# Extra TensorE products ahead of the gathered sums of a four-layer vision block

## The chip, the cores and the metric

The kernel is one program on one core of a Trainium2 chip. The metric is the device time of that core in microseconds (us), as the median of several runs. TensorE is called PE here, VectorE DVE, ScalarE ACT, GpSimd POOL and SyncE SP, as in the profile.

## The reference

Four images of 256 channels by 64x64 pixels, all in float32, go through four residual layers; ahead of each layer the image is normalised in groups of 8 channels (`_gn`).

```python
x = x + L0(_gn(x))   # 1x1 convolution, deformable 3x3 sampling (4 groups, 9 points), SE gate, MLP
x = x + L1(_gn(x))   # qkv, a 5x5 depthwise branch, linear attention, projection
x = x + L2(_gn(x))   # 3x3 convolution with binarised weights
x = x + L3(_gn(x))   # non-local attention over a 2x2 max-pooled image
```

The part that matters here is the sampling of layer 0. For each pixel, group and point the reference reads four neighbouring pixels at a computed place, weighs them bilinearly, multiplies by a softmax mask and adds the nine points:

```python
samp = _grid_sample(img, sg)                       # 4 corners x bilinear weights
dout = (samp * mask).sum(-1)                       # over the 9 points
dout = einsum('nhwc,oc->nhwo', dout, outproj_w)    # 1x1 projection, then a batch norm
```

## The kernel before

**Stages.** `run` (L1218) first convolves image 0, then runs four samplings, one an image, one after the other. Beside each sampling other work is laid in: beside the first (image 0) the convolutions and the sampling offsets of images 1 to 3 (`convolve`, `offsets`); beside the second the binarised weights, then `feedforward` and `layer1` of image 0; beside the third and the fourth `feedforward` and `layer1` of the image before, and `layer2` and `layer3` of the image two before. After the samplings comes what is left of the last images.

**A sampling** (`sample`, L558) goes in 16 blocks of 18 rounds, 288 rounds in all. In a round, `gathered` (L592) issues four indirect DMAs on POOL (one a group, L596, each with 128 rows of 256 floats into a tile `g`, of which there are seven), and 8 matmuls on PE (L603) that multiply the gathered rows with a sparse weight tile `wm` into `acc`. These 8 matmuls are "the sums". The profile has each float32 matmul twice, so a round's sums are 16 records there. `acc` is one PSUM bank: two halves of 256 columns, used in turn by pairs of rounds; an even round writes the first 128 columns of its half, the odd round the other 128.

After an odd round, ACT copies its half out (`moved`, L608, into `at`) in the next round; PE transposes it (`turned`, L613, into `dp`) in the round after that; ACT spreads it into `dT` (`spread`, L623). After a block, `project` (L636) makes 8 matmuls, two groups of 4, six to eight rounds later. ACT also makes the weight tiles `wm` (L588) for the rounds to come.

**The order** on PE, DVE, ACT and POOL is the order in which the program emits (`manual_schedule`). A helper, `beside` (L1234), takes one round of the sampling and then as much of the other work as is due, so a round's place on PE is: what is due of `turned` and `project`, the sums, then the other work that falls into this round. The first matmul of an even round's sums waits for ACT's copy of the pair before, since both are in the same PSUM bank.

```python
for i in range(NBLK * BR):
    b, r = divmod(i, BR)
    for f in later.pop(i, ()):
        f()
    if r % UR == 0:                       # UR = 2: a pair of rounds
        acc = next(accs)
    gathered(blocks[b], weights[0][0], acc, r)
```

Of the kernel before, what the change touches and what calls it, by code (L numbers as in the profile page):

```python
# [17 lines left out]
P = 128  # L18
# [24 lines left out]
STEPS = 900  # L43
CONV, SECOND = NB * 22.5 + 11, 568
# [27 lines left out]
class Net:  # L72
    def __init__(self, ctx, tc, a, out):
# [5 lines left out]
        self.banks, self.alone, self.spare = cycle(["mm"]), False, False  # L79
        self.dp = e(tc.tile_pool(name="scratch", bufs=1, space=DRAM))  # L80


# [29 lines left out]
    def groupnorm(self, pool, st, name):  # L112
# [7 lines left out]
        nc.tensor.matmul(pg[:, 0:KT], self.bd8, mv[:, :, 0], start=True, stop=True)  # L120
# [8 lines left out]
        nc.tensor.matmul(pv[:, 0:KT], self.bd8, d, start=True, stop=True)  # L129
# [6 lines left out]
    def folded(self, pool, out, w, sc, bi, name):  # L136
# [5 lines left out]
        for m in range(n):  # L142
            for k in range(KT):
                nc.tensor.matmul(ps[:, m:m + 1], w[:, k, m * P:(m + 1) * P], bi[:, k:k + 1], start=k == 0, stop=k == KT - 1)
# [109 lines left out]
    def binarise(self):  # L254
# [4 lines left out]
        with self.tc.tile_pool(name="bin", bufs=1, side="left") as sp, \  # L259
# [17 lines left out]
            for i in range(6):  # L277
                nc.tensor.matmul(ps[:, 0:C], self.ones, sums[:, i], start=i == 0, stop=i == 5)
# [27 lines left out]
    def weights(self, pool):  # L306
# [7 lines left out]
        for m in range(KT):  # L314
            dg = pool.tile([P, P], F32, name=f"dg{m}")
            nc.vector.tensor_scalar(dg, self.ident, self.inv[:, m:m + 1], None, ALU.mult)
            nc.tensor.matmul(ps[:, m * P:(m + 1) * P], self.ones, dg, start=True, stop=True)
# [4 lines left out]
    def convolve(self, n, w, sp, bp, pads, used):  # L322
# [47 lines left out]
        def convolved(b, x, yb, m):  # L370
            ps = self.ps1.tile([P, 512], F32, name="cv", tag="vk")
            for k in range(KT):
                nc.tensor.matmul(ps, cw[:, k, m * P:(m + 1) * P], x[:, k], start=k == 0, stop=k == KT - 1)
# [13 lines left out]
        def projected(b, x, yb, xo, j2):  # L387

            ps = self.ps().rearrange("p (r o) -> p r o", o=C)
            for r in range(2):  # L390
                for h in range(2):
                    at = (4 * h + 2 * j2 + r) * W
                    for k in range(KT):
                        nc.tensor.matmul(ps[64 * h:64 * h + 64, r], yb[:, k, at:at + W], w["iw"][:, k], start=k == 0, stop=k == KT - 1)
# [81 lines left out]
    def offsets(self, n, c, y, mw, bp, used):  # L476
# [14 lines left out]
        for h in range(2):  # L491
            ps = self.ps().rearrange("p (j o) -> p j o", o=P)
            for j in range(4):
                at = (4 * h + j) * P
                for k in range(KT):
                    nc.tensor.matmul(ps[:, j, 0:3 * Q], t[:, k, at:at + P], mw[:, k], start=k == 0, stop=k == KT - 1)
# [61 lines left out]
    def sample(self, n, ssum):  # L558
# [33 lines left out]
        def gathered(sl, wm, acc, r):  # L592
# [8 lines left out]
            for x in range(2):  # L601
                for i in range(G):
                    nc.tensor.matmul(acc[32 * i:32 * i + 32, :], wm[:, r4, 4 * i + 2 * x:4 * i + 2 * x + 2, :],  # L603
# [29 lines left out]
        def project(b, m):  # L633
            po[m] = self.ps("po")
            for k in range(G):
                nc.tensor.matmul(po[m][:, 0:BR * OB], self.ow[:, k, m * P:(m + 1) * P], dT[b][:, k].rearrange("p r o -> p (r o)"), start=k == 0, stop=k == G - 1)  # L636
# [19 lines left out]
        for i in range(NBLK * BR):  # L656
# [3 lines left out]
            if r % UR == 0:  # L660
                acc = next(accs)
            gathered(blocks[b], weights[0][0], acc, r)
            if r == 0 and b + 1 < NBLK:
# [22 lines left out]
    def feedforward(self, n, ssum, st):  # L686
        nc, tc, a = self.nc, self.tc, self.a
        with tc.tile_pool(name=f"fa{n}", bufs=1, side="right") as sp, \
# [13 lines left out]
            for k in range(KT):  # L702
                nc.tensor.matmul(ps[0:64, 0:1], sd[:, k], mean[:, k:k + 1], start=k == 0, stop=k == KT - 1)
# [4 lines left out]
            for m in range(KT):  # L708
                ps = self.ps()
                nc.tensor.matmul(ps[:, 0:1], su[:, m * P:(m + 1) * P], dn, start=True, stop=True)  # L710
# [673 lines left out]
```

## Time and profile before

| | |
|---|---|
| median of 3 runs | 8691.39 us (8685.18 to 8699.55) |
| profiled execution, its own time | 8695.07 us |
| span of its profile | 8693.3 us |
| granted TensorE clock, mean over the span | 0.803 |
| sums of sampling 1 / 2 / 3 / 4 on PE | from about 140 / 1934 / 3659 / 5449 us, the last to 7210 us |
| busy in the span | PE 5880.0, DVE 4817.7, ACT 3541.0, POOL 4934.7 us |

The span is the time from the first to the last instruction of the profiled execution; the 1.8 us around it belong to that execution's own time. "PEclk" is the share of the full TensorE clock that was granted. A group's row has the busy time, the mean duration in ns, and the idle time of its engine just before it with what ended it. "remote" (in the chain: "another core or an unknown queue") is a wait whose releasing event has no instruction beside it in the records; as there is one core, it is no other core here. Samplings are counted from 1 in the text; in the code they are `n` = 0 to 3.

### The profile page before, as it was taken

The page shows a single profiled execution, that of the slowest core. Times are in us where ns is not written, and L with a number is a line of the kernel's source. Part 1 is how long each engine was busy: PE and PEld are TensorE (multiplying, and loading weights), DVE is VectorE, ACT ScalarE, POOL GpSimd, SP SyncE. Part 2 cuts the span into 40 slices and gives each one's busy share as a digit, 9 for nine tenths or more (in the row PEclk, how much of TensorE's full clock was granted, in tenths as well). Part 3 has the DMA queues.
Part 4 walks back from the last instruction along what each step waited for, and adds up shares of the span by engine and source line. Part 5 has one row for each costly group of instructions (what it writes and reads, how often), then busy time and mean ns, then how long its engine had stood idle before and what let it go on. Part 6 is the DMA issues. An engine that isn't in the chain of part 4 may idle for free.

```text
span 8693.3 us, 99761 instructions
## 1 busy us (share of the span) xinstructions
PE 5880.0 (68%) x35776; PEld 3498.6 (40%) x35776; DVE 4817.7 (55%) x6045; ACT 3541.0 (41%) x10767; POOL 4934.7 (57%) x4870
## 2 busy tenths in 40 slices
PE   4454554448744446688876676888766778986899
PEld 2232222224323222234644443345544333664476
DVE  5344442443366667324776675228766762699833
ACT  2333333234444433334445443444454442456414
POOL 2666666466666666666666556666655560476410
PEclk7676766669866667799988887999878879998899
DMA  6454554444533334444543344445433342220131
GB/s 172 129 160 123 145 149 118 114 143 148 158 107 106 110 109 126 137 127 138 142 133 111 111 116 138 146 135 142 141 105 111 112 118 96 74 72 29 44 97 54
DMA packets 744383, 1031.75 MB, mean 119 GB/s; under 512 B 354128, under 2 KB 459984, under 8 KB 742352
## 3 DMA queue, kind: packets, MB, share of 16 engines
q0 software_dynamic: 221184, 604.27, 24.4%
q1 hardware_dynamic: 522704, 421.10, 16.4%
q8 instruction: 283, 4.64, 0.2%
q14 instruction: 212, 1.74, 0.1%
HBM read 856.39 MB, written 168.61 MB: 118 GB/s over the span
## 4 chain that ended last, share of the span: by engine, by line
PE 43%; another core or an unknown queue 17%; DVE 17%; ACT 13%; issue 8%; DMA 1%; POOL 0%; SPq 0%; ACTq 0%; DVEq 0%; POOLq 0%
DVE agg L178 10%; PE acc L603 6%; PE ps L739 5%; PE ps L749 5%; ACT wm L588 5%; PE ps L1085 4%; PE ps L821 3%; PE ps L943 2%; PE ps L1203 2%; PE s L1185 2%; PE po L636 2%; ACT dT L623 2%; ACT at L608 1%; PE rden L934 1%
## 5 line engine op out<-in xcount | busy, mean ns | idle before, releaser
L596 POOL DMA_INDIRECT g<-tab,sl x4608 | 4399.0, 955 | 2790.8 <-issue 1179.7
L178 DVE SCALAR_TENSOR_TENSOR agg<-pad,vec,agg 128x1024 f32<-128x1024 f32 x2280 | 2934.5, 1287 | 63.9
L603 PE MATMUL acc<-g,wm 128*32 128x128 f32 x18432 | 1012.4, 336 | 2022.6 <-ACT at L608 1471.8
L603 PEld LDWEIGHTS acc<-g,wm 128*32 128x32 f32 x18432 | 557.7, 129 | 2524.7 <-ACT at L608 1683.4
L588 ACT ACTIVATE wm<-sl,con 128x48 f32<-128x48 f32 x6144 | 1490.1, 366 | 26.0 <-remote 12.6
L1085 PE MATMUL ps<-xd,w 128*128 128x256 f32 x3072 | 741.0, 392 | 37.6 <-issue 30.1
L623 ACT COPY dT<-dp 64x128 f32<-64x128 f32 x1152 | 297.2, 258 | 985.8 <-remote 524.3
L1085 PEld LDWEIGHTS ps<-xd,w 128*128 128x128 f32 x3072 | 587.3, 196 | 159.0 <-issue 79.0
L739 PE MATMUL ps<-x2f,f 128*128 128x512 f32 x1024 | 502.3, 639 | 10.2 <-issue 5.1
L608 ACT COPY at<-acc 128x256 f32<-128x256 f32 x576 | 214.5, 372 | 712.8 <-remote 607.4
L821 PE MATMUL ps<-xr,qw 128*128 128x512 f32 x768 | 463.5, 733 | 21.8 <-issue 8.5
L724 DVE SCALAR_TENSOR_TENSOR hm<-ps,vec,lk 128x512 f32<-128x512 f32 x256 | 190.6, 750 | 502.4 <-ACT lk L741 375.2
L749 PE MATMUL ps<-hm,f 128*128 128x512 f32 x1024 | 463.6, 601 | 0.0
L741 ACT ACTIVATE lk<-ps,low 128x512 f32<-128x512 f32 x256 | 174.0, 687 | 514.7 <-PE ps L739 413.2
L636 PE MATMUL po<-dT,ow 128*128 128x288 f32 x1024 | 336.7, 477 | 56.5 <-issue 13.8
L875 ACT COPY kt<-pt 128x512 f32<-128x512 f32 x256 | 149.5, 585 | 544.8 <-remote 246.8
L1036 POOL TENSOR_TENSOR xd<-xp 128x640 f32<-128x640 f32 x64 | 79.8, 1275 | 497.3 <-DMA xq<-x 280.3
L1203 PE MATMUL ps<-gt,pT 128*128 128x129 f32 x2048 | 316.5, 315 | 47.1 <-ACT pT L1199 32.9
L613 PE MATMUL dp<-ident,at 128*128 128x128 f32 x1152 | 285.5, 336 | 77.1 <-ACT dT L623 53.4
L1203 PEld LDWEIGHTS ps<-gt,pT 128*128 128x128 f32 x2048 | 297.2, 226 | 98.8 <-ACT pT L1199 45.0
L1185 PE MATMUL s<-ph,th 128*128 128x512 f32 x512 | 289.2, 677 | 42.9 <-DVE ot L938 9.2
L739 PEld LDWEIGHTS ps<-x2f,f 128*128 128x128 f32 x1024 | 199.2, 203 | 253.3 <-issue 238.5
(243 smaller groups left out, 7710.6 us busy)
## 6 DMA issues: line engine op xcount, KB each, us to landing
g<-tab,sl POOLq DMA_INDIRECT x4608
x<-x SPq DMA_DIRECT2D x128, 512.0 KB
xr<-x SPq DMA_DIRECT2D x96, 512.0 KB
tab<-xo SPq DMA_DIRECT2D x192, 128.0 KB
x<-in_x SPq DMA_DIRECT2D x32, 512.0 KB
y<-yc SPq DMA_DIRECT2D x32, 512.0 KB
yb<-y SPq DMA_DIRECT2D x64, 256.0 KB
x<-yb SPq DMA_DIRECT2D x64, 256.0 KB
```

The source lines that it names most:

```text
L178: nc.vector.scalar_tensor_tensor(to, s, wt, acc, ALU.mult, ALU.add)
L588: nc.scalar.activation(wm[:, :, :, o], blocks[b][:, r:r + WR, G:], AF.Copy, scale=self.con("own")[:, o:o + 1])
L596: nc.gpsimd.indirect_dma_start(out=g[:, i, :], out_offset=None, in_=table, in_offset=bass.IndirectOffsetOnAxis(ap=sl.bitcast(I32)[:, r, i: ...
L603: nc.tensor.matmul(acc[32 * i:32 * i + 32, :], wm[:, r4, 4 * i + 2 * x:4 * i + 2 * x + 2, :], g[:, i, x * P:(x + 1) * P], start=x == 0, st ...
L623: nc.scalar.copy(dT[b][hs, :, r:r + UR], dp[u][hs, :, :, s, :].rearrange("p v g o -> p g v o"))
L636: nc.tensor.matmul(po[m][:, 0:BR * OB], self.ow[:, k, m * P:(m + 1) * P], dT[b][:, k].rearrange("p r o -> p (r o)"), start=k == 0, stop=k ...
L739: nc.tensor.matmul(ps, f1[:, k, m * P:(m + 1) * P], x2[:, k], start=k == 0, stop=k == KT - 1)
L749: nc.tensor.matmul(ps, f2[:, k, m * P:(m + 1) * P], hm[:, k], start=k == 0, stop=k == 4 * KT - 1)
L821: nc.tensor.matmul(ps, qw[:, k, m * P:(m + 1) * P], x[:, k], start=k == 0, stop=k == KT - 1)
L1085: nc.tensor.matmul(ps[:, e], w[:, k, t, 2 * half + e, m * P:(m + 1) * P], v[:, 2 * half + e, k, t:t + 8], start=i % 6 == 0, stop=i % 6 == 5)
L1185: nc.tensor.matmul(s[i], tv[:, 4 * b + j], ph[:, i * 512:(i + 1) * 512], start=True, stop=True)
L1203: nc.tensor.matmul(ps[:, 0:P + 1], pT[:, m], gt[:, m], start=m == 0, stop=m == 7)
```

## The change

A counter `self.work` adds up the PE work that is emitted: a helper `of` wraps the output of every `matmul` call (not of the transposes) and adds twice its columns, scaled by the share of the 128 partitions that it writes. In the first two samplings (`n < 2`), ahead of a round's sums, PE multiplies the constant identity matrix with a part of the constant weight tile `ow`, into the part of `acc` from the round's own columns to the end of its half, until the counter has reached `ALIVE = 2048`. The sums then overwrite these values. After the sums the counter is set to 0. So a round in which other work of 2048 or more was emitted since the last sums gets no extra product, and a round with none gets 2048 of it: 4 products of 256 columns in an even round (512 each), 8 of 128 columns in an odd one (256 each).

```diff
+ALIVE = 2048
...
-        self.banks, self.alone, self.spare = cycle(["mm"]), False, False
+        self.banks, self.alone, self.spare, self.work = cycle(["mm"]), False, False, 0
...
+    def of(self, out):
+
+        self.work += 2 * out.size() // P
+        return out
...
-                nc.tensor.matmul(ps, cw[:, k, m * P:(m + 1) * P], x[:, k], start=k == 0, stop=k == KT - 1)
+                nc.tensor.matmul(self.of(ps), cw[:, k, m * P:(m + 1) * P], x[:, k], start=k == 0, stop=k == KT - 1)
...
             if r % UR == 0:
                 acc = next(accs)
+            while n < 2 and self.work < ALIVE:
+                free = acc[:, r % UR * P:]
+                nc.tensor.matmul(self.of(free), self.ident, self.ow[:, 0, 0:free.shape[1]], start=True, stop=True)
             gathered(blocks[b], weights[0][0], acc, r)
+            self.work = 0
```

The third line pair stands for the same edit at every other `matmul` call of the kernel; it emits nothing of its own.

## The prediction

> **What bounds the kernel now.** I read the page first, for the clock.
>
> ```profile
> PEclk7676766669866667799988887999878879998899
> ```
>
> Each digit is one fortieth of the span (217 us). Slices 1 to 9 and 12 to 16, the first sampling and the later part of the second, have 6 or 7 tenths of the clock; from slice 19 on it is mostly 8 or 9. The table by stage says more (columns: stretch, its length, busy time of PE, weight loads, DVE, ACT and POOL with instruction counts, clock, DMA share, GB/s).
>
> ```profile
> 280.00:1900.00 1620.00, 773.00 (x6110) 437.94 (x6102) 663.87 (x936) 549.53 (x2042) 1007.48 (x1048) 0.67 0.48 135
> 2000.00:2400.00 400.00, 311.51 (x1742) 152.11 (x1741) 148.72 (x220) 172.69 (x572) 252.62 (x261) 0.89 0.49 150
> 2400.00:3600.00 1200.00, 630.66 (x4518) 341.95 (x4518) 797.84 (x757) 466.41 (x1658) 779.94 (x822) 0.68 0.40 112
> ...
> 4400.00:5300.00 900.00, 616.64 (x4205) 381.34 (x4202) 652.66 (x748) 425.26 (x1345) 536.28 (x565) 0.82 0.41 120
> ```
>
> In the first sampling (first row) PE is busy 773 of 1620 us at clock 0.67, and no other engine is full: POOL 62%, DVE 41%, ACT 34%. So it is bound by waits. The chain of waits, cut to the samplings 1, 2 and 3, says which:
>
> ```profile
> by line: another core or an unknown queue 39.9%; ACT wm L588 9.8%; issue 9.5%; DVE agg L178 7.3%; PE acc L603 4.9%; PE ps L496 3.5%; PE cv L373 2.7%; PE ps L394 2.7%; ACT dT L623 2.2%; ACT at L608 1.8%; PE po L636 1.6%; ACT t L484 1.1%; PE
> by line: another core or an unknown queue 28.5%; ACT wm L588 8.3%; PE acc L603 7.9%; issue 7.9%; PE ps L739 6.8%; PE ps L749 6.2%; PE ps L821 4.2%; PE ps L943 3.1%; ACT dT L623 2.7%; DVE agg L178 2.5%; PE po L636 2.4%; ACT at L608 2.4%; PE
> by line: DVE agg L178 11.5%; another core or an unknown queue 8.8%; PE acc L603 8.0%; issue 7.8%; PE ps L739 6.1%; PE ps L749 5.9%; PE ps L1085 5.7%; PE ps L821 5.0%; PE ps L943 3.5%; ACT wm L588 2.9%; PE s L1185 2.8%; PE ps L1203 2.8%; PE
> ```
>
> The unknown queue holds 39.9% of 1794 us = 716 us in sampling 1, 28.5% of 1725 us = 492 us in sampling 2, and only 8.8% of 1790 us = 158 us in sampling 3. What it is, the timeline shows:
>
> ```profile
> 864.87 1.08 PE L603 MATMUL acc<-g,wm 128*32 128x128 f32 x16
> ...
> 876.83 0.37 ACT L608 COPY at<-acc 128x256 f32<-128x256 f32 x1 [8.59 <-remote]
> ...
> 877.26 1.08 PE L603 MATMUL acc<-g,wm 128*32 128x128 f32 x16 [11.31 <-ACT at L608]
> ```
>
> The odd round's sums are issued from 864.87 and their records end at 865.95, yet ACT's copy of them starts at 876.83, after 8.59 us of idle ACT, and PE's next sums start behind the copy after 11.31 us. PE tells of its end some 10 us late. I read the unknown queue as such late ends of PE work; what makes them late the trace doesn't tell. POOL and the sums in samplings 1 and 2 (busy, mean ns | idle before, by releaser):
>
> ```profile
> L596 POOL DMA_INDIRECT g<-tab,sl x1168 | 1123.4, 962 | 672.2 <-issue 311.5 <-remote 211.5 <-PE acc L603 120.0
> L603 PE MATMUL acc<-g,wm 128*32 128x128 f32 x4608 | 305.7, 370 | 871.5 <-ACT at L608 569.1 <-issue 267.1 <-DMA g<-tab,sl 22.5
> L596 POOL DMA_INDIRECT g<-tab,sl x1163 | 1110.4, 955 | 611.2 <-issue 299.9 <-remote 148.3 <-PE acc L603 99.9
> L603 PE MATMUL acc<-g,wm 128*32 128x128 f32 x4608 | 258.0, 353 | 592.8 <-ACT at L608 476.6 <-issue 86.0 <-ACT lk L741 12.5
> ```
>
> POOL waits 672.2 - 311.5 = 361 us and 611.2 - 299.9 = 311 us for more than its own issue gap, mostly for PE to free a `g` tile. A round takes 1794/288 = 6.2 and 1725/288 = 6.0 us; POOL alone needs 4 x (955 + about 300 ns) = 5.0 us. So PE and ACT in their turn set the pace, and POOL follows up to seven rounds ahead.
>
> **What the skill says.** The Trainium skill, "TensorE: Matmul & The Clock Gate", section "Part 1: The HAM clock gate", says that the array runs at half clock by default, that a window of about 3.4 us with sustained activity gives the full clock, and that an idle window takes it away. The trace agrees, and is sharper. Consecutive windows of 3.41 us (second number after the length: PE busy; then the same columns as above):
>
> ```profile
> 854.07:857.49 3.42, 1.82 (x17) 1.10 (x18) 0.00 (x0) 2.22 (x9) 2.62 (x3) 0.50 0.58 174
> 857.49:860.90 3.41, 3.41 (x10) 1.22 (x12) 0.00 (x0) 0.00 (x0) 2.03 (x3) 0.50 0.36 97
> 860.90:864.31 3.41, 1.20 (x33) 0.73 (x33) 0.00 (x0) 1.57 (x7) 1.44 (x2) 1.00 0.16 44
> ...
> 901.86:905.27 3.41, 3.41 (x19) 1.65 (x20) 0.00 (x0) 3.41 (x15) 2.50 (x4) 0.50 0.26 77
> 905.27:908.69 3.42, 1.76 (x20) 0.66 (x18) 0.00 (x0) 0.82 (x4) 1.01 (x2) 1.00 0.26 77
> 908.69:912.10 3.41, 2.35 (x32) 1.60 (x32) 1.62 (x2) 3.07 (x10) 2.77 (x3) 1.00 0.27 77
> ```
>
> At 0.50 a window with 1.82 us of PE work is followed by 0.50, full ones (3.41 us) by 1.00; at 1.00 a window with 1.76 us of work keeps it, and the 1.20 us of 860.90 lose it. Half clock needs twice the time for the same work, so both say: about 1.5 us of full-clock work in 3.4 us. I go by this. The second page is "PSUM — Partial Sum Buffer", section "Terms": two engines must not be in one bank and quadrant at once. The wait shown above (sums behind the copy) is its price here: PE's sums waited 569.1 us for L608 in sampling 1. The extra products of an even round write the same bank, so they stand behind the same wait and cannot fill it.
>
> **The change, part by part.** (1) The counter emits nothing: 0 us. (2) *How many products.* I went through PE's order from sums to sums and added up 2 x columns x partitions/128 of each matmul between. Roughly checked by groups: in sampling 1 L394 (384 matmuls x 256), L373 (96 x 1024), L496 (240 x 216) and L636 (120 x 576) make 317,600, or 1,100 a round, in lumps: 152 of 288 rounds have none, 112 have 2048 or more. Sampling 1 gets products in 176 rounds: 327 of 256 columns and 658 of 128. Sampling 2: 152 rounds, 247 and 506. (3) *Price of one.* No row is the same product; the nearest by columns are these, whose busy time per record is the pace in a dense stretch near full clock:
>
> ```profile
> L1085 PE MATMUL ps<-xd,w 128*128 128x256 f32 x3072 | 741.0, 392 | 37.6 <-issue 30.1
> ...
> L1203 PE MATMUL ps<-gt,pT 128*128 128x129 f32 x2048 | 316.5, 315 | 47.1 <-ACT pT L1199 32.9
> ```
>
> 741.0/3072 = 0.241 us a record, two records: 0.48 us for 256 columns. 316.5/2048 = 0.155, so 0.31 us for 128 columns (L1203 has 129). At full clock: sampling 1, 327 x 0.48 + 658 x 0.31 = 361 us; sampling 2, 247 x 0.48 + 506 x 0.31 = 276 us. At half clock twice that: 722 and 551 us. I take a fifth of it at half clock, since a lump of products fills a window: 433 and 331 us.
>
> (4) *How much of it is on the path.* PE is idle about half the time, but the products come behind the copy and ahead of the sums; queued behind them on PE are the sums, then the laid-in matmuls and transposes, and ACT's copy, DVE, and POOL's gather seven rounds on wait for those. Of the sums' busy time the chain holds 4.9% of 1794 = 88 of 305.7 us (0.29) in sampling 1, and 7.9% of 1725 = 136 of 258.0 us (0.53) in sampling 2. The work just ahead of the sums is on the path in the same share: 433 x 0.29 + 331 x 0.53 = 126 + 175 = 301 us. Where it is hidden, PE's idle time hides it; with no cover the price is 764 us.
>
> (5) *What the clock gives back.* A round of 6 us holds 1.8 windows. At least 2048 of extra or other work (4 records of 512 columns; the chain has 16 such records of L749 in 7.06 us, so 1.8 us) plus the sums (0.65 us for 16 records at full clock in the timeline) make 2.4 us a round, or 1.4 us a window: near what the rows above need, so some windows turn and some don't. I estimate the clock to go from 0.65 to about 0.76 in sampling 1 and from 0.74 to 0.82 in sampling 2. PE work on the chain (sums, L496, L373, L394, L636: 15.4% of 1794 = 276 us; in sampling 2 sums, L739, L749, L821, L943, L636: 30.6% of 1725 = 528 us) shrinks by about 14% and 10%: 39 + 53 = 92 us.
>
> (6) No DMA is added, and SP and POOL get no instruction; the gathers keep their order on POOL. Samplings 3 and 4 and the rest are as before: 0 us. The late ends (716 + 492 us) I leave as they are, because the trace has them inside full-clock windows too. Their bounds are the first and third rivals.
>
> Sum: 8695 + 301 - 92 = 8904 us against the profiled execution's own time; that is 4 us above the median, so 8900 us.
>
> **Rivals.**
> *Late ends go away (faster).* By stage they are rare where PE is dense: 158 us of the chain in sampling 3, whose row 4400 to 5300 has clock 0.82. If the products bring the first two samplings there, up to 716 + 492 - 2 x 158 = 892 us leave the chain, but POOL cannot gain more than the 361 + 311 = 672 us that it waits. A quarter to a half of that gives 8691 - 168 = 8520 to 8691 - 336 = 8355 us; I take 8480. For it: density and late ends go together from stage to stage. Against: the late end shown follows a PE that had worked, and within sampling 1 I find no fewer behind busier stretches.
> *All hidden.* The products fall into PE's idle half and the clock pays for the rest: 8691 us. Against: even rounds have them behind the copy.
> *The clock stays low (the change doesn't do what it says).* The products stand in one lump, windows between lumps are empty; half clock all through: 722 x 0.29 + 551 x 0.53 = 501, so 9190 us. The same comes out if PE's slow stretches stay: at 919 to 926 us its timeline has single L496 matmuls 0.7 to 1.4 us apart with no wait; 16 records at 0.7 us are 11 us a round, and 45 such rounds of 328 add 500 us. It decides from some 20 such rounds on.
>
> **How the numbers follow.** The priced case has 0.42, the costlier one 0.12, hidden 0.06, late ends gone 0.40. The likeliest is the priced one, 8900 us; its own range is 8760 (full-clock prices 105 + 146, and twice the gain from the clock) to 9190. As both signs hold much of the chance, the range for 8 in 10 goes from 8390, inside the faster case, to 9200. A measurement of this kernel can tell about 0.2% (17 us) from no change. Faster by more 0.40, within 0.06, slower 0.54.
>
> **What the profile of the changed kernel would show.** 1970 and 1506 new records of the product; clock by stage 0.76 and 0.82; the chain's unknown share in samplings 1 and 2 about as now, with the new line holding some 7 to 10%; rounds of about 6.6 us. I am wrong if the unknown share falls to a tenth and POOL's waits with it (faster), or if rounds stay at 6.0 to 6.2 us with the products in PE's idle time.

## The result and the profile after

| kernel | median of 5 runs | ratio to before, 95% interval |
|---|---|---|
| before | 8699.55 us (8685.18 to 8707.84) | |
| changed | 8741.12 us (8729.55 to 8747.68) | 1.0048 [1.0035, 1.0061] |

The change costs 42 us, 0.5%. The forecast had the sign right and the size five times too large (8900 us, +209). The profiled execution took 8729.55 us with a span of 8727.8 us. In the changed kernel the lines have moved: the products are L670, the sums L609 (before L603), the gathers L602 (L596), ACT's copy L614 (L608), `wm` L594 (L588), the spreads `dT` L629 (L623), DVE's `agg` L184 (L178).

The clock on the page of the changed kernel, by fortieths of the span:

```profile
PEclk8787877779988788799988787999888878998899
```

Slices 1 to 16 went from mostly 6 and 7 to mostly 7 and 8, with some 9. The table by stage for the stretches shown in the prediction (samplings 1, 2 and 3; same columns):

```profile
280.00:1900.00 1620.00, 1040.88 (x7765) 701.28 (x7765) 663.93 (x939) 546.23 (x2031) 1000.92 (x1043) 0.79 0.48 135
2400.00:3600.00 1200.00, 811.75 (x5826) 532.98 (x5829) 800.11 (x755) 462.33 (x1638) 767.59 (x809) 0.81 0.39 111
4400.00:5300.00 900.00, 621.99 (x4286) 393.32 (x4285) 650.70 (x743) 425.14 (x1345) 540.15 (x569) 0.83 0.41 118
```

PE is busy 1041 us in place of 773 in the first row, the clock is 0.79 in place of 0.67, and yet POOL issued 1043 gathers in these 1620 us, against 1048 before. PE did a third more, and POOL's pace hardly changed. The chain of waits for samplings 1, 2 and 3:

```profile
by line: another core or an unknown queue 36.4%; PE acc L670 9.6%; ACT wm L594 9.0%; issue 8.1%; PE acc L609 6.1%; DVE agg L184 5.5%; PE ps L502 3.9%; PE cv L379 3.2%; ACT dT L629 1.9%; ACT at L614 1.9%; PE ps L400 1.7%; PE po L642 1.4%; PE
by line: another core or an unknown queue 20.9%; PE acc L670 9.9%; issue 8.6%; PE acc L609 8.0%; PE ps L749 6.5%; PE ps L759 6.3%; DVE agg L184 6.0%; ACT wm L594 5.4%; PE ps L831 4.6%; PE po L642 2.7%; PE ps L953 2.4%; ACT dT L629 2.2%; ACT
by line: issue 15.1%; DVE agg L184 10.8%; another core or an unknown queue 8.7%; POOL g L602 6.8%; PE acc L609 6.6%; PE ps L1095 5.9%; PE ps L749 4.8%; PE ps L831 3.9%; PE ps L759 3.2%; PE s L1195 3.1%; PE ps L1213 2.8%; ACT wm L594 2.5%; P
```

The new line L670 holds 9.6% of 1794 = 172 us and 9.9% of 1725 = 171 us, 343 us in all. In the same stretches the unknown queue fell from 716 to 653 us and from 492 to 361 us, together by 194 us. The groups of sampling 1, from its first to its last gather (busy, mean ns | idle before, by releaser):

```profile
L602 POOL DMA_INDIRECT g<-tab,sl x1152 | 1106.6, 961 | 812.8 <-issue 299.4 <-remote 210.6 <-DMA sl<-sd 138.5
L670 PE MATMUL acc<-ow,ident 128*128 128x128 f32 (+1 forms) x1922 | 456.1, 401 | 313.4 <-ACT at L614 229.3 <-issue 79.4 <-ACT dT L629 4.7
L609 PE MATMUL acc<-g,wm 128*32 128x128 f32 x4512 | 267.5, 320 | 259.7 <-ACT at L614 141.4 <-issue 96.2 <-DMA g<-tab,sl 16.2
L614 ACT COPY at<-acc 128x256 f32<-128x256 f32 x141 | 52.5, 373 | 458.4 <-remote 364.3 <-PE acc L609 66.6 <-PE cv L379 13.7
```

The same view of the kernel before:

```profile
L603 PE MATMUL acc<-g,wm 128*32 128x128 f32 x4512 | 298.6, 370 | 854.4 <-ACT at L608 554.5 <-issue 264.5 <-DMA g<-tab,sl 22.5
L608 ACT COPY at<-acc 128x256 f32<-128x256 f32 x140 | 52.2, 373 | 421.5 <-remote 391.8 <-PE ps L394 9.9 <-PE acc L603 9.8
```

Before the change PE waited 554.5 us for the copy and 264.5 us on issue ahead of the sums, 819 us. After it, PE waited ahead of products and sums together 229.3 + 141.4 us for the copy and 79.4 + 96.2 us on issue, 546 us. So 273 of the 456 us of products came out of this waiting. From the first gather of sampling 1 to the first of sampling 2, PE's idle time fell from 958 to 652 us in all, its other work from 813 to 672 us at the higher clock, and the sampling grew by 10 us. ACT's copy meanwhile waits as ever for an end that comes late (391.8 and 364.3 us). Where the wait went is to be seen in one stretch of the changed kernel's timeline:

```profile
902.46 0.44 PE L619 MATMUL dp<-ident,at 128*128 128x128 f32 x2
...
902.73 1.95 PE L670 MATMUL acc<-ow,ident 128*128 128x128 f32 x16
...
905.50 0.95 POOL L602 DMA_INDIRECT g<-tab,sl  x1 [0.30 <-issue]
...
907.46 0.38 PE L609 MATMUL acc<-g,wm 128*32 128x128 f32 x3 [1.69 <-issue]
...
908.25 0.53 ACT L629 COPY dT<-dp 64x128 f32<-64x128 f32 x2 [5.96 <-remote]
908.44 0.95 POOL L602 DMA_INDIRECT g<-tab,sl  x1 [2.00 <-remote]
```

PE's transposes (L619) end at 902.90. ACT, which needs only them, starts at 908.25, after 5.96 us of idle time. In between PE runs 16 records of products for 1.95 us that ACT does not wait for, then sums with gaps of up to 1.69 us that the trace puts down to issue. POOL's last gather ends at 906.45, POOL stops for 2.00 us, and 1.8 us into that stop ACT is told of PE's end. POOL's next gather (908.44) waits for the same semaphore, the one that PE counts up at its ends. So this stretch leaves open which comes first: POOL's stop may let the end through, or an end that is late for another reason may release both. The experiments follow this.

From here on, the *lateness* of a PE end is the time from the modelled end of a PE instruction's record to the start of an ACT or DVE instruction whose wait it ended and whose engine was idle when that record ended; a *stop* is more than 0.45 us between two gathers on POOL. Both are worked out from the records. Which waits are counted changes the size of the lateness (the expectations have 3.95 us for sampling 1 of the kernel before, this count 3.24), but not the order of the kernels below.

### The profile page after: what moved, and what is told of

Its sections match the earlier page's. It is cut to its first block, busy times and chain, and to the rows that moved or that the text cites. A ratio compares the mean times of both kernels' runs of the same rounds, so it can differ in the third digit from the quotient of the medians.

```text
span 8727.8 us, 106573 instructions
## 1 busy us (share of the span) xinstructions
PE 6409.0 (73%) x39260; PEld 4017.6 (46%) x39260; DVE 4816.4 (55%) x6045; ACT 3540.5 (41%) x10767; POOL 4939.4 (57%) x4870
## 4 chain that ended last, share of the span: by engine, by line
PE 47%; DVE 16%; another core or an unknown queue 15%; ACT 12%; issue 8%; POOL 2%; DMA 1%; SPq 0%; ACTq 0%; DVEq 0%; POOLq 0%
DVE agg L184 9%; PE acc L609 6%; PE ps L1095 6%; PE ps L749 5%; PE ps L759 4%; ACT wm L594 4%; PE acc L670 4%; PE ps L831 3%; PE ps L1213 2%; PE s L1195 2%; PE ps L953 2%; PE po L642 2%; POOL g L602 1%; ACT dT L629 1%
## 5 line engine op out<-in xcount | busy, mean ns | idle before, releaser
L602 POOL DMA_INDIRECT g<-tab,sl x4608 | 4404.2, 956 | 2826.2 <-issue 1168.6
L184 DVE SCALAR_TENSOR_TENSOR agg<-pad,vec,agg 128x1024 f32<-128x1024 f32 x2280 | 2934.4, 1287 | 63.9
L609 PE MATMUL acc<-g,wm 128*32 128x128 f32 x18432 | 957.2, 315 | 1037.5 <-ACT at L614 733.2
L594 ACT ACTIVATE wm<-sl,con 128x48 f32<-128x48 f32 x6144 | 1488.6, 365 | 21.6 <-DMA sl<-sd 11.8
L609 PEld LDWEIGHTS acc<-g,wm 128*32 128x32 f32 x18432 | 527.4, 122 | 1537.2 <-ACT at L614 888.6
L670 PE MATMUL acc<-ow,ident 128*128 128x128 f32 (+1 forms) x3484 | 816.0, 396 | 523.8 <-ACT at L614 403.8
L670 PEld LDWEIGHTS acc<-ow,ident 128*128 128x128 f32 x3484 | 652.1, 249 | 630.4 <-ACT at L614 442.1
L629 ACT COPY dT<-dp 64x128 f32<-64x128 f32 x1152 | 297.2, 258 | 1014.6 <-remote 504.8
L614 ACT COPY at<-acc 128x256 f32<-128x256 f32 x576 | 214.4, 372 | 744.5 <-remote 549.2
L831 PE MATMUL ps<-xr,qw 128*128 128x512 f32 x768 | 429.1, 687 | 14.0 <-ACT pT L1209 5.2
L619 PE MATMUL dp<-ident,at 128*128 128x128 f32 x1152 | 266.9, 318 | 86.7 <-ACT dT L629 60.9
```

The lines of the kernel that those rows point to most:

```text
L184: nc.vector.scalar_tensor_tensor(to, s, wt, acc, ALU.mult, ALU.add)
L594: nc.scalar.activation(wm[:, :, :, o], blocks[b][:, r:r + WR, G:], AF.Copy, scale=self.con("own")[:, o:o + 1])
L602: nc.gpsimd.indirect_dma_start(out=g[:, i, :], out_offset=None, in_=table, in_offset=bass.IndirectOffsetOnAxis(ap=sl.bitcast(I32)[:, r, i: ...
L609: nc.tensor.matmul(self.of(acc[32 * i:32 * i + 32, :]), wm[:, r4, 4 * i + 2 * x:4 * i + 2 * x + 2, :], g[:, i, x * P:(x + 1) * P], start=x ...
L629: nc.scalar.copy(dT[b][hs, :, r:r + UR], dp[u][hs, :, :, s, :].rearrange("p v g o -> p g v o"))
L670: nc.tensor.matmul(self.of(free), self.ident, self.ow[:, 0, 0:free.shape[1]], start=True, stop=True)
```

## Experiments

Theories at the start: **W**, the products cost their share of PE's path, and by making PE's work denser they shorten the late ends, so the two nearly cancel. **H**, something else sets the pace of a round, and the products fall into time in which PE would have waited. In the runs with fewer gathers or rows (e5, e6, e10, e11, e12) the sums of groups 3 and 4 read the rows of groups 1 and 2 in samplings 1 and 2; the other rows are left out there, and these kernels do not compute the reference's result. The runs of one series shared one chip and the runs of the kernel before; the series were on five chips.

### Series 1: where and what the products are (before: 8680.37 us)

**e1_odd: odd rounds only.**

```diff
-            while n < 2 and self.work < ALIVE:
+            while n < 2 and r % UR and self.work < ALIVE:
```

> Products only in odd rounds of samplings 1 and 2 (1172 of the 1742 products, all of 128 columns, 371 of the 816 us that they keep PE busy). These stand behind the even round's sums and not behind ACT's copy. Theory W (work: products cost time on PE's path and, by making PE denser, shorten the late ends, the two nearly cancel): about half of each, net +10 to +30 us on the kernel before (8700), unknown share of the chain down from 716 + 492 to about 610 + 430 us. Rival C (the cost sits in the even rounds, whose products wait for the copy, and the gain comes from both): 8600 to 8670. Rival H (products only take the place of waiting time, one for one): 8700, chain's unknown share lower by just what the products hold.

Measured 8723.44 us, 1.0043 [1.0032, 1.0054].

**e2_even: even rounds only.** As above with `r % UR == 0`.

> Products only in even rounds of samplings 1 and 2 (570 products of 256 columns, 445 of the 816 us), all behind ACT's copy of the pair before. Theory W: +10 to +30 us on the kernel before. Rival C (even rounds carry the cost): +60 to +130 us. Rival H: within 20 us of the kernel before, with the unknown share lower by the products' share.

Measured 8715.32 us, 1.0034 [1.0024, 1.0043]. Each half alone costs nearly as much as both (+37 and +30 us by ratio, against +42): the cost is not a sum over products, and neither kind is the cheap or the dear one. Rival C falls. No theory's range holds the first number (H: no change, W: +10 to +30); the second is at W's upper end and outside H's 20 us.

**e3_mm: the products of even rounds in another bank.**

```diff
+            free = self.ps("free")[:, 0:256] if n < 2 and self.work < ALIVE and r % UR == 0 else acc[:, r % UR * P:]
             while n < 2 and self.work < ALIVE:
-                free = acc[:, r % UR * P:]
```

> As the changed kernel, but the products of an even round go into a bank of the rotation of three that the other matmuls use, so that they need not wait for ACT's copy and can run while PE waits for it. Theory W: the products of even rounds (about 170 to 200 us of the 343 us that the products hold on the chain) leave the path, PE's work and clock stay as in the changed kernel: 8560 to 8640, below both kernels. Rival L (the late ends come whatever PE does in between, and the copy's wait is already as long as the late end): as the changed kernel less what ran behind the copy, 8640 to 8700. Rival B (the rotation of three banks is what other matmuls wait for): slower than the changed kernel, 8760 or more, with new waits on the rotation's readers.

Measured 8725.54 us, 1.0049 [1.0035, 1.0063], the same as the changed kernel. The even products no longer wait for the copy (PE is idle 43.1 us ahead of them, against 505.1 us in the changed kernel), and nothing is gained by it, although they still hold 6.1% and 3.0% of the chain in samplings 1 and 2. So their wait for the copy was not what set the time. All three expectations missed the number; it fits H.

**e4_thin: the same number of products with 2 columns.**

```diff
-                nc.tensor.matmul(self.of(free), self.ident, self.ow[:, 0, 0:free.shape[1]], start=True, stop=True)
+                nc.tensor.matmul(self.of(free)[:, 0:2], self.ident, self.ow[:, 0, 0:2], start=True, stop=True)
```

> As many products, in the same places, but each with 2 columns in place of 256 or 128: the instructions are there and the work is not. Theory W (density of work and the clock shorten the late ends): clock and unknown share as in the kernel before (0.65 / 0.74; 716 + 492 us), time 8690 to 8740 with the price of 1742 short instructions. Rival I (a PE instruction's end is told sooner when other instructions follow it, whatever their size): unknown share down by 150 us or more at no gain in clock, 8500 to 8620.

Measured 8739.23 us, 1.0069 [1.0043, 1.0094]. The groups of this kernel have a surprise:

```profile
L670 PE MATMUL acc<-ow,ident 128*128 128x2 f32 x3484 | 713.9, 330 | 554.7 <-ACT at L614 493.9 <-issue 51.0 <-ACT dT L637 5.9
```

and so has its table by stage:

```profile
280.00:1900.00 1620.00, 1083.79 (x7776) 769.70 (x7775) 664.34 (x939) 546.43 (x2033) 998.96 (x1042) 0.66 0.48 135
2400.00:3600.00 1200.00, 897.16 (x5829) 630.13 (x5821) 800.35 (x755) 463.22 (x1644) 765.75 (x811) 0.63 0.38 111
```

A record with 2 columns occupies PE for 713.9/3484 = 0.205 us, no less than one with 128: from start to start of two products the median is 0.213 us at half clock and 0.112 us at full clock with 2 columns, and the same 0.213 and 0.112 us with 128 columns in the changed kernel. So the test of instructions without work became another test: PE just as occupied (1084 us), the clock as low as before (0.66), and the time 0.2% from that of the changed kernel (1.0069 [1.0043, 1.0094] and 1.0048 [1.0035, 1.0061] overlap). The chain of this run has 33.9% of 1794 = 608 us of unknown queue in sampling 1 and 17.7% of 1725 = 305 us in sampling 2, both less than the changed kernel's 653 and 361 us. So the unknown share shrinks without streamed work and without a higher clock, and W, which wanted it to stay at 716 + 492 us, falls in this form, though its time range (8690 to 8740 us) holds the number. Rival I had the share right (down by 295 us at no gain in clock) and the time wrong (8500 to 8620 us). Whether occupied time or the mere presence of later instructions shortens the share, this run can't separate. H stays.

### Series 2: half the gathers, more and fewer products (before: 7720.99 us)

The chip of this series ran the kernel before in 7721 us, 11% less than the one before it. Nothing here is compared across chips without saying so.

**e5_half_before, e6_half_after: two gathers a round in samplings 1 and 2.**

```diff
-            for i in range(G):
+            for i in range(2 if n < 2 else G):
                 nc.gpsimd.indirect_dma_start(
...
-                                     g[:, i, x * P:(x + 1) * P], start=x == 0, stop=x == 1)
+                                     g[:, i % 2 if n < 2 else i, x * P:(x + 1) * P], start=x == 0, stop=x == 1)
```

> The kernel before with two gathers a round in place of four in samplings 1 and 2 (the sums of groups 3 and 4 read the rows of groups 1 and 2, so half of the gathered rows is left out there). PE, ACT and DVE have the same instructions. Theory H (POOL's gathers and the late ends that come with them set the pace of a round; PE's products fall into the time that PE would have waited): samplings 1 and 2 shorten a lot, from 1772 and 1707 us to 1100 to 1450 each, unknown share of the chain below half (under 350 and 250 us). Theory W (PE and ACT in their turn set the pace, late ends come from thin PE work): samplings 1 and 2 stay within 10%, 1600 to 1770 us, unknown share about as before (700 and 490 us).

> The changed kernel with the same two gathers a round in samplings 1 and 2. To be read against the run with two gathers and no products. Theory H: with the cover gone the products cost what they hold on PE's path: the difference between the two is 200 to 400 us, against 42 us with four gathers. Theory W: the difference is as with four gathers, 0 to 80 us.

Measured 7077.59 us (0.9166 [0.9152, 0.9180]) and 7202.16 us (0.9322 [0.9307, 0.9336]). Samplings 1 and 2 took 997 and 1270 us, the first less than H's 1100 us. The products cost 125 us here, three times as much as on the first chip, less than the 200 us that H expected and more than W's 80 us.

**e7_4096, e8_1024: the amount.**

```diff
-ALIVE = 2048
+ALIVE = 4096        # e7_4096; ALIVE = 1024 in e8_1024
```

> ALIVE = 4096: 6277 products in place of 1742 (4535 more matmuls than the changed kernel). Theory H: PE has about 1000 us of waiting left in sampling 1 and 700 in sampling 2, so the cover runs out: some 1400 to 1700 us more PE work of which about 900 to 1200 is covered, 9000 to 9400. Theory W (price and shorter late ends nearly cancel at any amount): 8760 to 8900.

> ALIVE = 1024: 777 products in place of 1742. Theory H: the products are covered, what they cost is small and about in proportion: +10 to +25 us on the kernel before. Theory W: half the price and less than half the gain, +30 to +80 us; or, if the gain comes first, below the kernel before.

Measured 7901.65 us (1.0228 [1.0214, 1.0242]) and 7724.77 us (1.0003 [0.9995, 1.0011]). With 4096 the profile has 9070 records of L670, so 4535 products in all; the 6277 of the expectations of e7_4096 and e14_4096 count the changed kernel's 1742 twice. The first range, written for a kernel of 8691 us, can't be set against this chip, where they cost 181 us. The +4 us of e8_1024 are below H's 10 to 25 and W's 30 to 80. The groups of sampling 1 of e8_1024 say why this chip is faster:

```profile
L602 POOL DMA_INDIRECT g<-tab,sl x1150 | 1108.6, 964 | 355.0 <-issue 328.7 <-DMA g<-tab,sl 15.8 <-PE acc L609 6.9
...
L614 ACT COPY at<-acc 128x256 f32<-128x256 f32 x143 | 53.2, 372 | 299.8 <-PE acc L609 297.9
```

There is no "remote" in either row. The chain of this run, which the profile follows back to 1619 us, has no unknown queue at all; in its sampling 2 (1604 to 3072 us) POOL's row leads it:

```profile
by line: POOL g L602 26.2%; issue 17.4%; PE ps L759 7.9%; PE ps L749 7.7%; DVE agg L184 6.9%; DMA g<-tab,sl 5.6%; PE acc L609 5.3%; PE ps L831 3.2%; PE po L642 2.3%; PE ps L953 1.9%; PE acc L670 1.6%; ACT at L614 1.0%; PE dp L619 1.0%; ACT 
```

In sampling 1 the copy waits for the sums and for nothing else, and POOL issues its gathers in one row: 1108.6 + 355.0 = 1464 us, the length of the sampling (1466 us). The late ends are all but absent on this chip (mean lateness 0.07 us in sampling 1). Samplings 3 and 4, which have no products, took 1584 us each here and 1789 and 1786 us in the kernel before; from the last sums to the end the two kernels took 1479 and 1483 us. So the chips differ where there are gathers and not after them. Here PE is plainly ahead of POOL, and 777 products cost nothing that can be measured.

### Series 3: the same with late ends (before: 8687.71 us)

**e9_after: the changed kernel again.**

> The changed kernel once more, to see it on the chip of this call: the runs with two gathers came from a chip on which the kernel before took 7721 us in place of 8691 and whose profiles have no unknown queue in the chain. Theory H: where the late ends are there (kernel before near 8690), +30 to +55 us; where they are not (near 7720), the floor of samplings 1 and 2 is POOL's own row of gathers (1111 us busy + 350 us between them = 1461 us) and PE is ahead of it, so the products cost 0 to 40 us. Theory W: where the late ends are not there, there is nothing to shorten and the products cost their whole share of PE's path, +200 to +350 us.

Measured 8734.02 us, 1.0053 [1.0037, 1.0070], as in the first comparison.

**e10_half_before, e11_half_after: the edits of e5 and e6.**

> The kernel before with two gathers a round in place of four in samplings 1 and 2 (half of the gathered rows left out there). Where the late ends are there: theory H (they come with the gathers' traffic) has sampling 1 below 1400 us and its unknown share below 350 us; theory W (they come with thin PE work) has it within 10% of 1772 us. Where they are not there: as the run before, samplings 1 and 2 of 997 and 1270 us.

> The changed kernel with two gathers a round in samplings 1 and 2, to be read against the run with two gathers and no products. Without late ends: +125 us, as the runs before. With them: theory H, +100 to +300 us; theory W, 0 to +80 us.

Measured 7573.76 us (0.8714 [0.8694, 0.8734]) and 7663.50 us (0.8826 [0.8805, 0.8846]). The groups of sampling 1 of e10_half_before, for the rows shown of the kernel before:

```profile
L596 POOL DMA_INDIRECT g<-tab,sl x573 | 559.0, 976 | 499.6 <-PE acc L603 288.9 <-issue 117.0 <-remote 64.8
L603 PE MATMUL acc<-g,wm 128*32 128x128 f32 x4512 | 235.4, 329 | 348.4 <-ACT at L608 274.1 <-issue 26.1 <-ACT dT L623 19.8
L608 ACT COPY at<-acc 128x256 f32<-128x256 f32 x140 | 52.2, 373 | 96.3 <-remote 54.2 <-PE acc L603 32.9 <-PE ps L496 2.4
```

PE, ACT and DVE do the same work as in the kernel before, and the "remote" wait of the copy falls from 391.8 to 54.2 us, PE's issue gaps ahead of the sums from 264.5 to 26.1 us, sampling 1 from 1772 to 1063 us. The profile does not follow the chain of this run back into sampling 1, so H's unknown share for it can't be read. The chain of its sampling 2 has 2 us of unknown queue left, not among its first lines:

```profile
by line: DVE agg L178 48.5%; PE ps L749 8.9%; PE ps L739 8.6%; PE acc L603 4.4%; issue 4.3%; DVE agg L180 2.2%; PE ps L943 2.0%; PE po L636 1.8%; PE ps L821 1.5%; PE rden L934 1.1%; ACT wm L588 1.0%; DVE ot L938 0.9%; ACT at L608 0.9%; PE d
```

So most of the lateness comes with the gathers, and PE, with half of them, can run a sampling in 1063 us with all of its work. That is what the prediction had denied ("PE and ACT in their turn set the pace"). The products cost 90 us here: 62 in sampling 1, and 26 in sampling 2, where they hold 16.0% of 1316 = 210 us on the chain of e11_half_after and DVE's `agg` falls from 48.5% to 12.4%:

```profile
by line: PE acc L670 16.0%; DVE agg L184 12.4%; PE acc L609 10.3%; PE ps L759 8.7%; PE ps L749 8.4%; PE ps L831 5.9%; PE po L642 4.3%; issue 3.9%; ACT at L614 2.8%; ACT dT L629 2.4%; PE ps L953 2.2%; PE dp L619 2.1%; ACT wm L594 2.0%; PE pt
```

Again a large share of the chain, and a small part of it in the time. That the other engine was just behind is the likely reason. The 90 us lie between W's 80 and H's 100 us, in neither range.

### Series 4: what about the gathers, and how far the cover goes (before: 8686.95 us)

**e12_short: four gathers, two of them with 32 rows.** From e10_half_before:

```diff
-            for i in range(2 if n < 2 else G):
+            for i in range(G):
+                rows = 32 if n < 2 and i > 1 else P
                 nc.gpsimd.indirect_dma_start(
-                    out=g[:, i, :], out_offset=None, in_=table,
-                    in_offset=bass.IndirectOffsetOnAxis(ap=sl.bitcast(I32)[:, r, i:i + 1], axis=0))
+                    out=g[0:rows, i, :], out_offset=None, in_=table,
+                    in_offset=bass.IndirectOffsetOnAxis(ap=sl.bitcast(I32)[0:rows, r, i:i + 1], axis=0))
```

> The kernel before, with four gathers a round on POOL, of which the third and fourth fetch 32 rows in place of 128 in samplings 1 and 2 (the sums of groups 3 and 4 read the rows of groups 1 and 2). Where the late ends are there: if they come with the bytes moved, lateness of PE's ends falls from 3.95 us to under 1 us in sampling 1 and its length to between 1100 and 1500 us; if they come with POOL's row of 1152 gather instructions, lateness stays at 2 us or more and the length at 1600 to 1770 us. Where they are not there: sampling 1 is 1000 to 1466 us.

Measured 8688.30 us, 1.0002 [0.9991, 1.0014]: no change at all. In the groups of its sampling 1 the late ends are all there:

```profile
L597 POOL DMA_INDIRECT g<-tab,sl x1152 | 1065.7, 925 | 830.2 <-issue 309.9 <-remote 256.9 <-DMA sl<-sd 138.5
...
L609 ACT COPY at<-acc 128x256 f32<-128x256 f32 x140 | 52.1, 372 | 448.9 <-remote 408.8 <-PE acc L604 10.4 <-issue 10.1
```

The table by stage of this run has 105 GB/s in its last column, against 135 of the kernel before in the same stretch:

```profile
140.00:1934.00 1794.00, 833.74 (x6630) 475.35 (x6631) 713.50 (x1026) 605.92 (x2264) 1089.79 (x1178) 0.65 0.38 105
```

So with as many gather instructions and 37% fewer rows nothing changed, and with half as many instructions the lateness mostly went: what counts is POOL's row of instructions, not the bytes. The Trainium skill, "Perfetto Trace Analysis", section "DMA Instruction — SWDGE (GPSIMD)", says that the end which the profile gives for such a DMA is the end of writing its descriptors and not of moving the data. The trace agrees in so far as a quarter of the rows left the instruction nearly as long (median 0.87 us for 32 rows, 0.95 us for 128). What the 0.87 us consist of is not shown.

**e13_bufs4: four gather tiles.**

```diff
-            g = self.gp.tile([P, G, 256], F32, name="g", bufs=7)
+            g = self.gp.tile([P, G, 256], F32, name="g", bufs=4)
```

> The kernel before with four gather tiles in place of seven in all samplings, so POOL can be four rounds ahead of PE and no more. Where the late ends are there: if POOL's lead carries the sampling over them, each sampling is longer by 5% or more, 9000 to 9500 in all; if the lead only makes the stretches of traffic and with them the late ends longer, the time stays within 1%, 8600 to 8780, with shorter late ends. Where they are not there: 7720 to 7900.

Measured 8690.79 us, 1.0007 [0.9998, 1.0015]. POOL's lead is indifferent. The mean lateness in sampling 1 (2.88 us) is only a little less than with seven tiles (3.24 us), so the second half of the expectation fails: the lead does not make the late ends much longer either.

**e14_4096, e15_1024: the amounts, with late ends.**

> ALIVE = 4096, 6277 products, to be seen beside the kernel before on this chip (on the chip without late ends it was +2.3%). Where the late ends are there: theory H (the products fill time in which PE would have waited), less than a third of the 4535 more products' 1500 us shows, +80 to +400 us on the kernel before, with the chain's unknown share under 250 us in each sampling. Theory W: price and gain nearly cancel at any amount, 0 to +100 us.

> ALIVE = 1024, 777 products. Theory H: +5 to +25 us on the kernel before, with or without late ends (+4 us on the chip without). Theory W: +30 to +80 us, or a gain, where the late ends are there.

Measured 8890.00 us (1.0238 [1.0223, 1.0252]) and 8716.24 us (1.0033 [1.0021, 1.0045]). The 29 us of the 777 products are a little more than H's 5 to 25 and just under W's 30 to 80. For 4535 products, 2.6 times those of the changed kernel, samplings 1 and 2 grew by 90 and 89 us. L670 is busy 1625 us in this kernel; 203 us show, within H's 80 to 400 and outside W's 0 to 100. The cover begins to run out but still takes seven eighths. H's unknown share of under 250 us in each sampling came in sampling 2 (145 us) and not in sampling 1 (18.0% of 1794 = 323 us).

### Series 5: loosening the loop (before: 8681.27 us)

**e16_three: three rounds between copies.**

```diff
-RP, WR, UR, BG = 14, 3, 2, 2
+RP, WR, UR, BG = 14, 3, 3, 2
...
-            t = self.ps1.tile([P, 2, 256], F32, name=name, tag=name)
-            return cycle([t[:, 0], t[:, 1]])
+            t = self.ps1.tile([P, 512], F32, name=name, tag=name)
+            return cycle([t[:, 0:UR * P]])
...
-            g = self.gp.tile([P, G, 256], F32, name="g", bufs=7)
+            g = self.gp.tile([P, G, 256], F32, name="g", bufs=6)
...
-                todo = [(i + 1 + j + (j == 2 and r < UR) * (6 - 3), f) for j, f in enumerate(todo)]
+                todo = [(i + 1 + j + (j == 2 and r < UR) * (5 - 3), f) for j, f in enumerate(todo)]
```

> The kernel before with three rounds in place of two between ACT's copies of acc (and transposes and spreads of three rounds at once; six gather tiles in place of seven, since four were as good). The whole bank holds one set of three rounds. Theory S (each copy needs an end of PE, which is told when POOL stops, so POOL stops about once a copy): 96 copies in place of 144 a sampling, POOL's long waits down from 120 to 195 a sampling to below 100 in samplings 1 and 2, each sampling shorter by 3 to 8%, 8250 to 8550 in all where the late ends are there. Rival (POOL's pace does not hang on PE's ends): 8650 to 8720. Where they are not there (7720): 7650 to 7800.

Measured 8589.23 us, 0.9893 [0.9872, 0.9914]: faster than both kernels, by 92 us on this chip. But theory S missed in size and in its sign-post: POOL's waits of over 0.35 us went from 120 to 116 and from 150 to 137 in samplings 1 and 2, not below 100. The rival's range (8650 to 8720 us) missed too. The four samplings are 24, 16, 31 and 29 us shorter than in the profile of before, which is from another chip with late ends. Fewer copies help; that one told end per copy sets the number of stops is not shown.

**e17_three_products: the same with products.** The changed kernel with the edits of e16_three and

```diff
-                free = acc[:, r % UR * P:]
+                free = acc[:, r % UR * P:min(r % UR + 2, UR) * P]
```

> The changed kernel in the same form, products of up to 256 columns ahead of a round's sums until 2048 is reached. Theory S: PE's waiting is shorter now but not gone; +20 to +120 us on the form with three rounds and no products. Rival: as the form without products or below it, since the clock is higher.

Measured 8623.70 us, 0.9936 [0.9919, 0.9953]: 34 us above e16_three, within S's 20 to 120. This form has 1514 products in place of 1742, and they cost about what they cost in the form with two rounds.

### The runs side by side

Mean lateness of PE's ends in samplings 1 / 2 / 3, and the gathers that POOL issued between 280 and 1180 us:

| kernel | lateness, us | gathers |
|---|---|---|
| before | 3.24 / 1.43 / 0.70 | 602 |
| changed | 2.39 / 1.14 / 0.65 | 603 |
| e4_thin | 2.24 / 1.08 / 0.70 | 600 |
| e12_short | 3.14 / 1.28 / 0.71 | 604 |
| e14_4096 | 1.15 / 0.62 / 0.64 | 577 |
| e10_half_before | 0.73 / 0.15 / 0.74 | 475, of half as many |
| e7_4096 (chip without late ends) | 0.11 / 0.07 / 0.05 | 711 |
| e8_1024 (the same chip) | 0.07 / 0.05 / 0.05 | 711 |

In the kernel before, after the last gather (376 ends, to 8693 us) the mean is 0.05 us and the longest 0.11 us: within one execution the late ends stop with the gathers.

The gathers keep the same pace, 900/602 = 1.50 us each, whether PE is busy 456 us of these 900 (before), 596 (changed) or 621 (e4_thin). Lateness depends on PE's work too: it falls with more products, and in sampling 3, where PE has more to do, it is 0.70 us with the same number of gathers. But sampling 3 is no shorter for it (1789 us).

PE's time in samplings 1 and 2 together, in us:

| kernel | length | products | other PE work | PE idle |
|---|---|---|---|---|
| before | 3479 | 0 | 1832 | 1646 |
| changed | 3512 | 810 | 1555 | 1148 |
| e4_thin | 3518 | 708 | 1789 | 1022 |
| e14_4096 | 3658 | 1612 | 1319 | 726 |

In the changed kernel 498 of the 810 us of products came out of PE's idle time and 277 out of other work that the higher clock made shorter; 33 us of length remain. In e4_thin, without the clock, 624 of 708 us came out of idle time, and the length is nearly the same.

In sampling 1 of the kernel before, 64% of the ends that came over 1.5 us late were told within a stop of POOL, though stops take 20% of the time; of the changed kernel's 74%, with stops 21% of the time. They were told 2.0 and 1.9 us (medians) after the stop began. This does not show that a stop lets an end through: 120 of the 122 stops before, and 158 of 162 in the changed kernel, end with PE's own semaphore, so most stops are themselves waits for an end of PE.

## Why the prediction was right or wrong

**Counter, counts (1, 2): right.** 3484 records of L670 against 1970 + 1506 = 3476; 1970 of them in sampling 1 and 1514 in sampling 2.

**Price (3): right in sum.** L670 is busy 816 us against 433 + 331 = 764:

```profile
L670 PE MATMUL acc<-ow,ident 128*128 128x256 f32 x1140 | 445.3, 554 | 505.1 <-ACT at L614 403.8 <-issue 88.0 <-ACT dT L629 10.5
L670 PE MATMUL acc<-ow,ident 128*128 128x128 f32 x2344 | 370.6, 320 | 18.7 <-issue 18.6
```

A 128-column record took 370.6/2344 = 0.158 us, near the 0.155 of full clock and under the 0.186 with a fifth at half clock; a 256-column one 445.3/1140 = 0.39 us in place of 0.29. The two misses partly cancel, which is luck. That columns set the price holds between 128 and 256; e4_thin shows that it does not hold below (2 columns took as long as 128 at the same clock).

**Share on the path (4): right as a share, wrong as time.** The chain has 343 us of products against 301. But the sum added it as if nothing else had held those microseconds. In e3_mm the even products left the copy's wait without effect; in e11_half_after 210 us on the chain of sampling 2 made it 26 us longer. A share of the chain is a price only where nothing else would have held that time.

**Clock (5): right as a clock, worth little.** 0.78 and 0.84 (140 to 1934 and 1934 to 3659 us) against 0.76 and 0.82. The Trainium skill's "TensorE: Matmul & The Clock Gate", "Part 1: The HAM clock gate", has sustained activity over about 3.4 us give the full clock; the rule that the prediction worked out from it and from the trace served well. e4_thin narrows it: there PE is busy 1084 of 1620 us and the clock is 0.66, in the changed kernel 1041 us and 0.79, so busy time as the profile gives it is not what decides. Of the 92 us that were to come of the clock little shows in the time. The other PE work did get 277 us shorter, but e4_thin, without that, is only 0.2% slower, within the noise. (Its products keep PE busy for 708 us in place of 810, so the comparison is not clean.)

**Late ends left as they are (6): this step failed,** and with it the adding up of (4). It put the term at 0: the products were to come on top of an unchanged wait. The unknown share of the chain fell by 63 + 131 = 194 us, and PE's idle time in samplings 1 and 2 by 498 us. With the 194 us the sum is 8904 - 194 = 8710 us, near the 8729.55 us of the profiled execution, but that nearness is partly luck, since it still has the 92 us of (5). The reason behind the step failed too. The prediction read PE and ACT as setting the pace and POOL as following, since POOL waited for `g` tiles. In e10_half_before half of POOL's gather instructions are taken away, and the same PE work runs in 1063 us. The late ends come with POOL's row of gathers, PE waits on them, and so PE work of a few hundred us in that row is mostly covered.

**Rivals.** *All hidden* (8691 us, given 0.06) named the mechanism, products in PE's idle half, and missed by the 42 us that still show. Its counter-argument, that even rounds have the products behind the copy, fell with e3_mm. *Late ends go away* was right that the unknown share would shrink and that an end comes less late where PE is denser (3.24 to 2.39 us), but products took the place of the waits, and POOL's pace did not move. *The clock stays low* fell with the trace, and e4_thin, with a low clock, is 0.2% from the changed kernel.

**Still open.** What in POOL's gather instructions goes with PE's late ends; whether a stop of POOL lets an end through or only waits for it; why the ends come less late with more PE instructions; why one of the five chips does not have them, and whether it is the chip or its state at the time; and why 42 us remain: sampling 1 is 10 us longer and sampling 2 24 us, and already 777 products (e15_1024) cost 29 us.

## What to carry to other kernels

When a wait's releaser is unknown, find out first what it goes with, by halving one engine's instructions while all else stays: a share of the chain says who held the time, not what the time would be without it. Work added to an engine that waits on another's row is mostly covered while that wait lasts (here 42 of 816 us showed), so its share of the chain overstates its price. And when a kernel's time differs by a tenth between chips, look for the stages that differ: here those with gathers did, and the rest of 1480 us did not.

## What the runs showed of the hardware

- The same program took 8680 to 8688 us (medians) on four of the chips of the series and 7721 us on a fifth. What the traces show of the difference is ends of PE that are told late while POOL issues indirect gathers: mean lateness in sampling 1 of 3.24 us in the kernel before, and of 0.07 us on the fast chip, in a kernel with 777 products. After the last gather it is 0.05 us on both kinds.
- Where there are late ends, they go with the gather instructions and not with their bytes: 32 rows in place of 128 in half of them changed nothing in the time (lateness 3.14 us), half as many instructions took the lateness from 3.24 to 0.73 us.
- PE's own issue suffers in the same stretches: gaps ahead of the sums 264.5 us in sampling 1, 26.1 us with half the gathers.
- A float32 product with 128x128 weights and 2 columns takes PE as long as one with 128 columns: 0.213 us from start to start at half clock and 0.112 us at full clock (medians), for both.
- PE busy with 2-column products for 1084 of 1620 us had a mean clock of 0.66, and with 128 and 256 columns for 1041 us one of 0.79.
